# Choosing the eight largest by zeroing them and subtracting the rest on GpSimd, in a convolution, mixture-of-experts and attention kernel

## The chip, the cores and the metric

The kernel runs on one core of a Trainium2 chip. The metric is the device time of one execution in microseconds (us); lower is better. The core has five engines that run side by side, each through its own queue in order: TensorE (PE, with its weight loads shown as PEld), VectorE (DVE), ScalarE (ACT), GpSimd (POOL) and SyncE (SP, which here only starts DMAs). They wait for each other through semaphores.

## The reference, cut to what matters

The input is 32 images of 128 channels and 56 by 56 points. Layer 0 is a depthwise convolution with a mixture of eight experts; the change does not touch it. Layer 1 sees each image as 3136 tokens of 128 channels. It adds an attention over each token's own channels, then a feed-forward part in which each of 64 experts picks its own tokens:

```python
t = t + _L1_attn_ref(_ln_t(t), ...)
# _L1_ffn_ref, with E = 64 experts and K = 8:
logits = jnp.einsum('bsd,ed->bse', x, gate_w) + gate_b
probs = jax.nn.softmax(logits, axis=1)              # over the tokens of one image
vals, idx = jax.lax.top_k(probs.transpose(0, 2, 1), K)
topv = vals.transpose(0, 2, 1)
...
pooled = jnp.einsum('bked,bke->bed', gathered, topv)
...
outputs = outputs.at[jnp.arange(Bn)[:, None], flat_idx].add(weighted)
```

So for every image and expert the eight tokens with the largest probability are needed, with their probabilities, and nothing of the others. The kernel writes this as a mask of 64 by 3136 values per image: the probability where the token is among the eight, and zero elsewhere. The mask, turned by TensorE, weighs the sum over tokens (`pooled`), and it weighs the expert's output again when that is added to the tokens at the very end.

## The kernel before, in words

The attention stage ("block 1") takes 784 tiles of 128 tokens, one in each step of a loop over `k`. A group is 7 tiles, a pair of images is 7 groups, which is 49 steps, and there are 16 pairs. The order of the work on every engine is written out by hand: the objects `pe`, `ve`, `sc` and `gp` tie each instruction behind the one before it on its engine. In step k the text issues, among others:

- `ends` (DVE): two reductions over the keys of two tiles, in every second step; they need `keys` (PE) of those tiles.
- `quotients` (DVE): three small operations, in the other steps.
- `offsets` (DVE): the 128 by 2048 differences `s` of tile k; they need `pivots` (POOL), which makes `c` for two tiles from what `ends` left.
- `scores` (POOL): multiplies `s` of tile k in place. `exps` (ACT) of tile k-1, `values` (DVE: `ev`) and `sums_s` (PE) of tile k-2, `sums_ev` (PE) of tile k-3 follow.

Each step also has two half-steps, calls of `group_work`, one after `keys` and one at the end of the step. They issue the work on whole groups from the table `places`: loading a group's tokens (`load`, by SP), their squares and scaling (`head_*`), the projection (`tail_sum`, `tail_summed`), the turned rows with their squares (`tail_rows`), and the logits (`tail_logits` to `tail_turned`). A place is a number of half-steps counted from the group's first tile. `tail_turned` writes the logits of a pair of images into `lg`, 128 partitions (2 images by 64 experts) by 3136 tokens.

When a pair's logits are complete, the generator `choose` is started, and every half-step runs it up to its next `yield`. In the half-steps counted from its start it does: at 0 DVE takes the eight largest of each row (`max`, into `m8`) and the negated largest; at 2 ACT forms `pb`, the exponentials of `lg` minus the largest, with their sum; at 4 DVE takes the reciprocal, and `match_replace` puts `FAR` (-3e38) into `lg` where the eight values stand; at 6 ACT scales `pb`; at 8 DVE keeps `pb` only where `lg` is below half of `FAR` (one `scalar_tensor_tensor`), and SP stores the mask to DRAM (`mk_d`). From 10 on, ten parts follow, eight half-steps each: PE turns a part of the mask (`cm`), two half-steps later ACT scales it into `mT`, two later PE multiplies it with the tokens (`acc`), three later DVE adds the result into `pT`.

The small PSUM results of the group work and of `choose` share one tag, `tp`, with three buffers; so each of them can start only when the third one before it has been read. SBUF buffers that the change touches: `lg` and `pb` one each of 3136 values per partition, `sq` two (scratch output of the squares), `tr` five and `t2` two.

Of the kernel before, what the change touches and what calls it, by code (L numbers as in the profile page):

```python
# [8 lines left out]
F32 = mybir.dt.float32  # L9
I32 = mybir.dt.int32  # L10
U32 = mybir.dt.uint32
AF = mybir.ActivationFunctionType
ALU = mybir.AluOpType
# [4 lines left out]
P = 128  # L18
GJ = 7
GT = P * GJ  # L20
# [5 lines left out]
def conv_attn_hybrid_kernel(  # L26
# [24 lines left out]
    nc = tc.nc  # L51
    N, C, H, W = x.shape
    HW = H * W
# [15 lines left out]
    E2 = gate_w.shape[0]  # L69
# [14 lines left out]
    mk_d = dram.tile([N, E2, HW], F32, name="mk_d")  # L84
# [31 lines left out]
    def group_rows(d, g):  # L116
        return d[g * GT : (g + 1) * GT, :].rearrange("(j p) c -> p j c", p=P)
# [18 lines left out]
    def by_tile(t):  # L136
        return t.rearrange("c (j p) -> c j p", p=P)
# [61 lines left out]
    with tc.tile_pool(name="cv_c", bufs=1) as cc, tc.tile_pool(  # L199
        name="cv", bufs=3  # L200
# [3 lines left out]
        gp = cc.tile([C, KS, 2 * H], F32, name="gp")  # L204
# [4 lines left out]
        bias = cc.tile([P, C], F32, name="bias")  # L209
# [113 lines left out]
    with tc.tile_pool(name="rt_c", bufs=1) as cc, tc.tile_pool(  # L323
        name="rt", bufs=4
# [72 lines left out]
    with tc.tile_pool(name="sel", bufs=1) as se, tc.tile_pool(  # L397
        name="sel2", bufs=2
# [260 lines left out]
    with tc.tile_pool(name="sc_c", bufs=1) as cc, tc.tile_pool(  # L659
        name="sc", bufs=4  # L660
# [50 lines left out]
        pe, ve, ac = (InOrder(e) for e in (nc.tensor, nc.vector, nc.scalar))  # L711

        def load(g):
            pr, gl = divmod(g, GPP)
            ct = cts[g] = sc.tile([C, GT], F32, name="ct", bufs=5)
            xg = xgs[g] = sc.tile([C, GT], F32, name="xg", bufs=5)
            for im, px, col, n in segments(gl):
                nc.sync.dma_start(
                    xg[:, col : col + n],
                    x[2 * pr + im].rearrange("c h w -> c (h w)")[:, px : px + n],  # L720
                )
                nc.sync.dma_start(ct[:, col : col + n], conv_d[2 * pr + im, :, px : px + n])
# [91 lines left out]
    with tc.tile_pool(name="ex_w", bufs=2) as ew, tc.tile_pool(  # L814
        name="ex", bufs=3
# [37 lines left out]
        gp = InOrder(nc.gpsimd)  # L853
# [3 lines left out]
        for i, (e, b) in enumerate(blocks):  # L857
# [15 lines left out]
            xa, rows, n = got.pop(i)  # L873
# [48 lines left out]
    keep = ctx.enter_context(tc.tile_pool(name="keep", bufs=1))  # L922
    pT = keep.tile([C, E2, N], F32, name="pT")
    NT = NG * GJ
    FAR = -3.0e38
    with tc.tile_pool(name="at_c", bufs=1) as cc, tc.tile_pool(
        name="at", bufs=2
    ) as at, tc.tile_pool(name="at_p", bufs=2, space=PSUM) as atp:
# [6 lines left out]
            return atp.tile([P, 4, P], F32, name=name, tag="tp", bufs=3)  # L935


        wr = at.tile([C, 3 * C], F32, name="wr", tag="lg", bufs=1)
        nc.sync.dma_start(wr, w_qkv)
        ps = bank("p_w")[:, :3, :].rearrange("p a c -> p (a c)")  # L940
        nc.tensor.matmul(ps, turn, wr, start=True, stop=True)
# [41 lines left out]
        pe, ve, sc, gp = (InOrder(e) for e in (nc.tensor, nc.vector, nc.scalar, nc.gpsimd))  # L983

        def squares(src, ss):

            sq = at.tile([P, C], F32, name="sq", bufs=2)
            sc.activation(sq[:, : C - 1], src[:, : C - 1], AF.Square, accum_out=ss)


# [61 lines left out]
        trs, zrs, roots, qs_, oTs, t2s, us, lgt = ({} for _ in range(8))  # L1052
# [101 lines left out]


        def load(g):
            tr = trs[g] = at.tile([P, GJ, C], F32, name="tr", bufs=5)
            nc.sync.dma_start(tr, group_rows(t_d, g))

        def head_squares(g, j0, j1):  # L1160
# [53 lines left out]
        def tail_summed(g, j0, j1):  # L1214
            pr, gl = divmod(g, GPP)
            if j0 == 0:
                t2s[g] = at.tile([C, GT], F32, name="t2")
            t2, ps = t2s[g], held.pop(("t", g, j0))
            sc.activation(by_tile(t2)[:, j0:j1, :], ps[:, : j1 - j0, :], AF.Identity, bias=bp)
            if j1 == GJ:  # L1220
                for im, px, col, n in segments(gl):
                    nc.sync.dma_start(t2_d[2 * pr + im, :, px : px + n], t2[:, col : col + n])
# [44 lines left out]
        def tail_turned(g, j0, j1):  # L1267
            pr, gl = divmod(g, GPP)
            if gl == 0 and j0 == 0:
                lgt[pr] = at.tile([2 * E2, HW], F32, name="lg", bufs=1)  # L1270
            ps = held.pop(("g", g, j0))
            for im, px, col, n in segments(gl):
                c0, c1 = max(col, j0 * P), min(col + n, j1 * P)
                if c0 < c1:
                    e = slice(im * E2, (im + 1) * E2)
                    sc.activation(
                        lgt[pr][e, px + c0 - col : px + c1 - col],
                        ps.rearrange("p j t -> p (j t)")[e, c0 - j0 * P : c1 - j0 * P],
                        AF.Identity, bias=gb[e, :],
                    )  # L1280
            if j1 == GJ:
                aT = at.tile([GJ, P], F32, name="aT", bufs=2)
                sc.copy(aT, ps[:GJ, 3, :])
                nc.sync.dma_start(
                    al_d[g * GT : (g + 1) * GT].rearrange("(j p) -> j p", p=P), aT
                )
# [3 lines left out]
        def choose(pr):  # L1290
            lg = lgt.pop(pr)
            m8 = at.tile([2 * E2, 8], F32, name="fm8")
            ve.max(m8, lg)
            sm = at.tile([2 * E2, 3], F32, name="fsm")
            ve.tensor_scalar(sm[:, 0:1], m8[:, 0:1], -1.0, None, ALU.mult)
            yield
            yield
            pb = at.tile([2 * E2, HW], F32, name="pb", bufs=1)
            sc.activation(pb, lg, AF.Exp, bias=sm[:, 0:1], accum_out=sm[:, 1:2])
            yield  # L1300
            yield
            ve.reciprocal(sm[:, 2:3], sm[:, 1:2])
            ve.match_replace(lg, m8, lg, FAR)
            yield
            yield
            sc.activation(pb, pb, AF.Copy, scale=sm[:, 2:3])
            yield
            yield
            ve.scalar_tensor_tensor(pb, lg, 0.5 * FAR, pb, ALU.is_lt, ALU.mult)
            nc.sync.dma_start(mk_d[2 * pr : 2 * pr + 2].rearrange("n e t -> (n e) t"), pb)  # L1310
            yield
            yield
            for im in range(2):
                e = slice(im * E2, (im + 1) * E2)
                parts = [(gl, *s[1:]) for gl in range(GPP) for s in tile_parts(gl) if s[0] == im]
                px = 0
                for gi, (gl, j0, j1, p) in enumerate(parts):
                    u, r = us[pr * GPP + gl]
                    pn, nj = p.stop - p.start, j1 - j0
                    ps = atp.tile([P, GJ, E2], F32, name="cm", tag="tp", bufs=3)  # L1320
                    for j in range(nj):
                        pe.transpose(
                            ps[:pn, j, :], pb[e, px + j * pn : px + (j + 1) * pn], ident[e, e]
                        )
                    px += nj * pn
                    yield
                    yield
                    mT = at.tile([P, GJ, E2], F32, name="mT", bufs=1)
                    if p.start:
                        sc.copy(mT[p, :nj], ps[:pn, :nj])  # L1330
                    for j in range(nj):
                        sc.activation(
                            mT[p, j], mT[p, j] if p.start else ps[p, j], AF.Copy,
                            scale=r[p, j0 + j : j0 + j + 1],
                        )
                    yield
                    yield
                    ps = atp.tile([P, E2], F32, name="acc", tag="tp", bufs=3)
                    for j in range(nj):
                        pe.matmul(  # L1340
                            ps, u[p, j0 + j, :], mT[p, j, :], start=(j == 0), stop=(j == nj - 1)
                        )
                    yield
                    yield
                    yield
                    if gi == 0:
                        ve.tensor_copy(pT[:, :, 2 * pr + im], ps)
                    else:
                        ve.tensor_tensor(
                            pT[:, :, 2 * pr + im], pT[:, :, 2 * pr + im], ps, ALU.add  # L1350
                        )
                    yield
# [2 lines left out]

        first, last, whole = (0, 4), (4, GJ), ()
        places = [
            (-43, load, whole),
            (-27, head_squares, (0, 2)), (-26, head_squares, (2, 4)),
            (-25, head_squares, (4, 6)), (-24, head_squares, (6, GJ)),  # L1360
            (-15, head_scale, (0, 2)), (-14, head_scale, (2, 4)), (-13, head_scale, (4, GJ)),
# [60 lines left out]
    with tc.tile_pool(name="f_c", bufs=1) as cc, tc.tile_pool(  # L1422
        name="f", bufs=3
    ) as fp, tc.tile_pool(name="f_p", bufs=2, space=PSUM) as fps, tc.tile_pool(
        name="o", bufs=2
# [59 lines left out]
        nc.sync.dma_start(fo_d, so)  # L1485
        nc.sync.dma_start(outF[:E2], fo_d.rearrange("n e c -> e n c"))

        OC = 448
        for n in range(N):
            mk = op.tile([E2 + 1, HW], F32, name="mk")  # L1490
            nc.sync.dma_start(mk[:E2], mk_d[n])  # L1491
# [1 line left out]
            t2 = op.tile([C, HW], F32, name="to")  # L1493
            nc.sync.dma_start(t2, t2_d[n])
            ot = op.tile([C, HW], F32, name="oo", bufs=2)
            for c0 in range(0, HW, OC):
                ps = fps.tile([C, OC], F32, name="p_o", bufs=3)
                nc.tensor.matmul(ps, outF[:, n, :], mk[:, c0 : c0 + OC], start=True, stop=True)  # L1498
                nc.vector.tensor_tensor(ot[:, c0 : c0 + OC], t2[:, c0 : c0 + OC], ps, ALU.add)  # L1499
            nc.scalar.dma_start(out[n].rearrange("c h w -> c (h w)"), ot)  # L1500
# [30 lines left out]
```

## Time and profile before

| what | value |
|---|---|
| median of 3 runs | 10098.04 us (10097.11 to 10102.77) |
| the profiled execution, its own time | 9671.71 us |
| its span, first to last instruction | 9670.0 us |
| mean granted TensorE clock | 0.941 |
| attention stage, its steady part, 4500 to 9048 us | 4548 us |
| busy in it: PE, DVE, POOL, ACT | 4270.2, 4299.7, 4184.6, 3639.4 us |

The profile is of one execution, which was shorter than the three timed ones. In the profile nearly every operation of this stage has line L161, since the helper that ties the instructions together issues them; they are told apart by the names of their tiles. An entry such as `s<-s,q 128x2048` reads: writes `s`, reads `s` and `q`, on 128 partitions by 2048 elements. `[0.96 <-DVE s L161]` after an entry says that the engine stood idle for 0.96 us before it and that the end of DVE's work on `s` released it.

### The profile page before, as it was taken

What the parts mean: (1) busy time and instruction counts of PE and PEld (TensorE: products, weight loads), DVE (VectorE), ACT (ScalarE), POOL (GpSimd) and SP (SyncE); (2) the same over time, 40 slices, a digit from 0 to 9 for tenths busy, and PEclk for the clock granted to TensorE, in tenths of its full rate; (3) what the DMA queues carried; (4) which work ended last, traced back from release to release, by engine and by line L of the source; (5) the groups of instructions that cost most, each with busy time, mean ns of one, the idle gap of its engine ahead of it and who ended that gap; (6) DMA issues with size and microseconds to landing.
All of it is one profiled execution on the core that took longest, in us unless ns stands there. A gap on an engine that the chain in (4) does not pass through costs nothing. (4 is left out here: it accounts for less than half of the span.)

```text
span 9670.0 us, 165492 instructions
## 1 busy us (share of the span) xinstructions
PE 8710.9 (90%) x62536; PEld 7091.7 (73%) x62536; DVE 6485.0 (67%) x10965; ACT 5264.1 (54%) x13385; POOL 6776.2 (70%) x4884
## 2 busy tenths in 40 slices
PE   9999467777999999997999999999999999999888
PEld 3449445555766666666898888898888898888853
DVE  2127888885222222227999999999999999999423
ACT  1116633333333333336887778878787887778400
POOL 0002147777877778778999999999999999999300
PEclk9999789998999999999999999999999999999765
DMA  9984147775444444441000000000000000000389
GB/s 210 214 196 145 56 130 208 208 209 146 74 66 71 70 65 63 65 68 28 31 24 31 31 29 29 31 24 31 31 31 27 31 24 31 31 29 27 95 275 332
DMA packets 1019567, 849.92 MB, mean 88 GB/s; under 512 B 525876, under 2 KB 912247, under 8 KB 999250
## 3 DMA queue, kind: packets, MB, share of 16 engines
q1 hardware_dynamic: 464018, 479.57, 17.4%
q0 software_dynamic: 177664, 188.81, 10.9%
q10 hardware_dynamic: 377088, 170.96, 6.5%
q8 instruction: 495, 8.11, 0.4%
q14 instruction: 302, 2.47, 0.1%
HBM read 486.34 MB, written 353.64 MB: 87 GB/s over the span
## 5 line engine op out<-in xcount | busy, mean ns | idle before, releaser
L161 POOL TENSOR_TENSOR s<-s,q 128x2048 f32<-128x2048 f32 x784 | 3598.9, 4596 | 205.6 <-DVE s L161 172.3
L161 ACT ACTIVATE s<-s 128x2048 f32<-128x2048 f32 x784 | 1501.6, 1915 | 871.2 <-POOL s L161 867.3
L161 POOL DMA_INDIRECT t_d<-ys,xe x992 | 1530.6, 1543 | 408.6 <-issue 230.2
L161 DVE TENSOR_TENSOR s<-kv,c 128x2048 f32<-128x2048 f32 x784 | 1788.6, 2281 | 7.4 <-POOL c L161 7.4
L161 DVE TENSOR_TENSOR ev<-s,kv 128x2048 f32<-128x2048 f32 x784 | 1785.7, 2278 | 1.9 <-ACT s L161 1.9
L161 PE MATMUL sm<-ident,ev 128*128 128x128 f32 x12544 | 1544.0, 278 | 109.6 <-DVE ev L161 109.3
L161 PE MATMUL sm<-ident,s 128*128 128x128 f32 x12544 | 1531.2, 276 | 8.1 <-ACT s L161 8.1
L161 PEld LDWEIGHTS sm<-ident,ev 128*128 128x128 f32 x12544 | 1429.5, 144 | 124.0 <-DVE ev L161 121.5
L161 PEld LDWEIGHTS sm<-ident,s 128*128 128x128 f32 x12544 | 1412.9, 143 | 28.3 <-ACT s L161 8.6
L888 ACT ACTIVATE hT<-ph,b1t 128x512 f32<-128x512 f32 (+1 forms) x992 | 679.3, 685 | 1238.8 <-PE ph L884 1223.4
L899 DVE TENSOR_TENSOR ys<-py,b2t 128x512 f32<-128x512 f32 (+1 forms) x248 | 171.5, 692 | 1527.7 <-PE py L894 1441.2
L894 PEld LDWEIGHTS py<-w,hT 128*128 128x128 f32 x7936 | 956.8, 192 | 202.4 <-issue 92.1
L884 PE MATMUL ph<-xeT,w 128*128 128x512 f32 (+1 forms) x1984 | 923.3, 599 | 70.5 <-DVE xeT L880 70.5
L894 PE MATMUL py<-w,hT 128*128 128x128 f32 x7936 | 980.7, 277 | 0.1
L697 POOL DMA_INDIRECT xb_d<-xs,rd x784 | 766.2, 977 | 240.2 <-issue 202.3
L241 PE MATMUL cps<-xin,br 56*64 56x448 f32 x7168 | 683.0, 539 | 13.0 <-DVE br L235 11.2
L884 PEld LDWEIGHTS ph<-xeT,w 128*128 128x128 f32 x1984 | 349.2, 191 | 393.3 <-issue 293.7
L161 PE MATMUL pa<-rw,ct 128*128 128x256 f32 x1568 | 423.1, 414 | 204.8 <-DVE xs L161 204.8
L241 PEld LDWEIGHTS cps<-xin,br 56*64 56x64 f32 x7168 | 282.3, 132 | 413.0 <-issue 410.4
L161 PEld LDWEIGHTS pa<-rw,ct 128*128 128x128 f32 x1568 | 301.3, 204 | 337.1 <-DVE xs L161 249.5
L287 POOL MEMSET code<- 128x64 f32 x1 | 0.2, 151 | 692.3 <-DMA conv_d<-ot 692.3
L161 ACT COPY add<-px 128x512 f32<-128x512 f32 x224 | 119.1, 532 | 607.1 <-PE px L161 589.8
(327 smaller groups left out, 13794.5 us busy)
## 6 DMA issues: line engine op xcount, KB each, us to landing
ct<-conv_d SPq DMA_DIRECT2D x192, 448.0 KB
xin<-in_x_dram SPq DMA_DIRECT2D x256, 196.0 KB
conv_d<-ot ACTq DMA_DIRECT2D x512, 98.0 KB
t_d<-xs ACTq DMA_DIRECT2D x112, 448.0 KB
tr<-t_d SPq DMA_DIRECT2D x112, 448.0 KB
to<-t_d SPq DMA_DIRECT2D x32, 1568.0 KB
out_dram<-oo ACTq DMA_DIRECT2D x32, 1568.0 KB
xg<-in_x_dram SPq DMA_DIRECT2D x96, 448.0 KB
```

What stands on the lines that cost most here:

```text
L161: r = getattr(self.engine, name)(*a, **k)
L241: nc.tensor.matmul(pss[r][b * HP : (b + 1) * HP], br[rows, kw, :], xi[rows, b * NB : (b + 1) * NB, kw : kw + W], start=(kw == 0), stop=(kw ...
L287: nc.gpsimd.memset(code, -1.0)
L697: s = nc.gpsimd.indirect_dma_start(out=xb_d, out_offset=bass.IndirectOffsetOnAxis(ap=idx, axis=0), in_=row, in_offset=None, bounds_check=R ...
L884: nc.tensor.matmul(ph[:, :, :rows], w1[:, f * P : (f + 1) * P], xT[:, :, :rows], start=True, stop=True,)
L888: nc.scalar.activation(hT[:, f, :, :rows], ph[:, :, :rows], AF.Gelu, bias=b1t[:, f : f + 1])
L894: nc.tensor.matmul(py[:rows, j, :], hT[:, f, j, :rows], w2[:, f, :], start=(f == 0), stop=(f == NF - 1),)
L899: nc.vector.tensor_tensor(ys[:rows], py[:rows], across(b2t, SB)[:rows], ALU.add)
```

## The change

The choice is made on the probabilities instead of the logits. ACT puts the eight largest values `m8` through the same exponential and the same scaling as `pb`. DVE's `match_replace` then reads `pb` and writes into `lg` a copy of `pb` in which the eight are zero. GpSimd subtracts that copy from `pb`, in seven parts of 448 columns, which leaves the eight probabilities and zeros. The parts are spread over the half-steps: two before the first part of the mask is turned, the others in pairs just after PE's turns. The store to `mk_d` follows the seventh. DVE's `scalar_tensor_tensor` is gone.

The order inside `choose`, in half-steps from its start, becomes: `max` 0, exponentials 2, reciprocal 4, scaling 5, `match_replace` 7, subtractions at 9, 10, 11, 12, 19, 20 and 27, and the ten parts from 11 on, one half-step later than before. `lg` now has two buffers, as it is read for longer. To make room, `sq` and `t2` have one buffer and `tr` four, and `load` is issued 30 half-steps ahead of its group instead of 43.

```diff
-    FAR = -3.0e38
+    OC = 448
...
-        wr = at.tile([C, 3 * C], F32, name="wr", tag="lg", bufs=1)
+        wr = at.tile([C, 3 * C], F32, name="wr", tag="lg", bufs=2)
...
-            sq = at.tile([P, C], F32, name="sq", bufs=2)
+            sq = at.tile([P, C], F32, name="sq", bufs=1)
...
-            tr = trs[g] = at.tile([P, GJ, C], F32, name="tr", bufs=5)
+            tr = trs[g] = at.tile([P, GJ, C], F32, name="tr", bufs=4)
...
-                t2s[g] = at.tile([C, GT], F32, name="t2")
+                t2s[g] = at.tile([C, GT], F32, name="t2", bufs=1)
...
-                lgt[pr] = at.tile([2 * E2, HW], F32, name="lg", bufs=1)
+                lgt[pr] = at.tile([2 * E2, HW], F32, name="lg", bufs=2)
...
             sc.activation(pb, lg, AF.Exp, bias=sm[:, 0:1], accum_out=sm[:, 1:2])
+            sc.activation(m8, m8, AF.Exp, bias=sm[:, 0:1])
             yield
             yield
             ve.reciprocal(sm[:, 2:3], sm[:, 1:2])
-            ve.match_replace(lg, m8, lg, FAR)
+            yield
+            sc.activation(pb, pb, AF.Copy, scale=sm[:, 2:3])
+            sc.activation(m8, m8, AF.Copy, scale=sm[:, 2:3])
             yield
             yield
-            sc.activation(pb, pb, AF.Copy, scale=sm[:, 2:3])
+            ve.match_replace(lg, m8, pb, 0.0)
             yield
             yield
-            ve.scalar_tensor_tensor(pb, lg, 0.5 * FAR, pb, ALU.is_lt, ALU.mult)
-            nc.sync.dma_start(mk_d[2 * pr : 2 * pr + 2].rearrange("n e t -> (n e) t"), pb)
-            yield
-            yield
+
+            def leave(i):
+
+                if i < HW // OC:
+                    at_ = slice(i * OC, (i + 1) * OC)
+                    gp.tensor_tensor(pb[:, at_], pb[:, at_], lg[:, at_], ALU.subtract)
+                if i == HW // OC - 1:
+                    nc.sync.dma_start(mk_d[2 * pr : 2 * pr + 2].rearrange("n e t -> (n e) t"), pb)
+
+            left = 0
+            while left < 2:
+                leave(left)
+                left += 1
+                yield
...
                     px += nj * pn
+                    leave(left)
+                    left += 1
                     yield
+                    leave(left)
+                    left += 1
                     yield
...
-            (-43, load, whole),
+            (-30, load, whole),
```

More of the change, by code (lines that the diff above doesn't have):

```diff
@@ L924, in conv_attn_hybrid_kernel @@
     NT = NG * GJ
-    FAR = -3.0e38
+    OC = 448
+    assert HW % OC == 0
     with tc.tile_pool(name="at_c", bufs=1) as cc, tc.tile_pool(
@@ L1486, in conv_attn_hybrid_kernel @@
         nc.sync.dma_start(outF[:E2], fo_d.rearrange("n e c -> e n c"))
-        OC = 448
         for n in range(N):
```

## The prediction

> **What bounds the kernel now.** I read the busy times by stretch first. The attention stage's steady part (columns: stretch and length, then busy time and instructions of each engine, granted TensorE clock, DMA share, GB/s):
>
> ```profile
> 4500.00:9048.00 4548.00, 4270.19 (x35134) 4026.30 (x35132) 4299.72 (x3755) 3639.38 (x9057) 4184.57 (x2417) 0.98 0.08 28
> 5649.00:5943.00 294.00, 273.30 (x2239) 257.19 (x2238) 274.47 (x241) 233.34 (x583) 267.12 (x156) 0.98 0.08 29
> ```
>
> The second line is one pair of images. DVE works 274 us of 294, PE 273, POOL 267: three engines near full, none alone the bound. DMA is idle. Pairs last 286.5 and 293.8 us in turn (from one `max` to the next), 290.2 in the mean.
>
> Then the waits, between 5000 and 8000 us (total, times, longest):
>
> ```profile
> ACT s L161 <- POOL s L161: 544.2, 326, 4.5
> DVE kx L161 <- PE kv L161: 139.5, 129, 5.7
> POOL s L161 <- DVE s L161: 120.3, 156, 3.5
> PE sm L161 <- DVE ev L161: 77.1, 32, 3.8
> ```
>
> Nearly all of DVE's idle time, 13.5 us a pair, is `ends` waiting for PE's keys. So away from the choice PE is the last to come. The fourth line shows the reverse, and the timeline places it: PE waits for `ev` where `choose` runs. There DVE is dense and PE and POOL are not:
>
> ```profile
> 5080.00:5106.00 26.00, 19.99 (x142) 18.71 (x141) 25.86 (x22) 19.27 (x52) 21.25 (x9) 0.89 0.26 98
> ```
>
> In this stretch lie `match_replace` and `scalar_tensor_tensor`. The timeline of DVE and POOL around the latter (start, duration, instruction):
>
> ```profile
> 5095.07 2.28 DVE L161 TENSOR_TENSOR s<-kv,c 128x2048 f32<-128x2048 f32 x1
> 5097.27 3.41 DVE L161 SCALAR_TENSOR_TENSOR pb<-lg,pb 128x3136 f32<-128x3136 f32 x1
> 5100.60 2.28 DVE L161 TENSOR_TENSOR ev<-s,kv 128x2048 f32<-128x2048 f32 x1
> ```
> ```profile
> 5091.85 4.58 POOL L161 TENSOR_TENSOR s<-s,q 128x2048 f32<-128x2048 f32 x1 [0.65 <-DVE s L161]
> 5097.50 7.60 POOL L161 TENSOR_TENSOR s<-s,q 128x2048 f32<-128x2048 f32 x1 [1.07 <-DVE s L161]
> ```
>
> Two prices stand here. On DVE the operation takes 5100.60 - 5097.27 = 3.33 us of the queue. And the product on GpSimd that starts beside it takes 7.60 instead of 4.58 us: 3.02 us lost. In the next pair a small product, `c<-q,kx`, takes 3.87 instead of 0.62: 3.25 lost. It is so in all 15 pairs that have work beside them. Beside `max` and `match_replace`, as long but with one input, the products keep 4.5 to 4.6 us.
>
> The last reading is PE's clock after such a gap:
>
> ```profile
> 5963.00:5968.00 5.00, 4.94 (x26) 4.57 (x27) 4.93 (x5) 4.87 (x5) 1.49 (x2) 0.66 0.23 92
> 5968.00:5977.00 9.00, 6.66 (x59) 6.18 (x57) 9.00 (x7) 8.78 (x35) 8.84 (x5) 1.00 0.16 68
> 5977.00:5982.00 5.00, 4.83 (x23) 4.37 (x23) 4.93 (x6) 1.45 (x1) 4.85 (x2) 0.66 0.50 206
> ```
>
> Twice per choice the granted clock falls to half for 3.4 us, once after PE's gap at `match_replace`, once after that at `scalar_tensor_tensor`.
>
> **What the Trainium skill says.** "SBUF — State Buffer", SBUF: two separate sides: a DVE operation with two SBUF inputs and a GpSimd operation that reads SBUF exclude each other for a whole instruction. The 3.0 to 3.25 us above agree; none of DVE's other operations here has two SBUF inputs (their second one is in PSUM), so the subtractions will not be locked out. "GPSIMD Engine Reference", Elementwise — side-by-side cycle accounting: a two-input product of 2048 columns takes 4497 ns on GpSimd, 2293 on DVE; the trace has 4569 (median) and 2281. "TensorE: Matmul & The Clock Gate", What's actually happening: an idle window of about 3.4 us halves PE's clock; the trace shows halves of 3.41 us, after gaps of 2.4 to 3.8 us.
>
> **The change part by part**, per pair, of which 16 are computed and 15 have other work beside them.
>
> *DVE loses `scalar_tensor_tensor`*: -3.33 us. DVE is dense there and PE waits for it (2.45 us idle in that step, 0.9 in the next), so I count it in full: 15 x 3.33 = -50 us. `max` and `match_replace` stay at 3.4 us each; the latter reads `pb` instead of `lg`, same size. What is late next is PE's own work.
>
> *The clock*: without that gap the second halving should go. It costs at most half of 3.41 us, 1.7 us a pair; PE may be hidden behind DVE meanwhile, so I take half, 0.85 x 15 = -13 us, bounds 0 and -26.
>
> *GpSimd gains seven subtractions of 448 columns.* From 0.62 us at 256 columns and 4.56 at 2048: 2.20 ns a column, 1.04 us each, 7.3 us a pair, 7.8 with the issue gaps. The lock's 3.0 to 3.25 us go, so POOL has 4.3 us more: 267 becomes 271 of 290, still under PE's 273. But they come in a bunch. With c the step in which the choice starts, one follows `scores` of step c+4, two that of c+5, one that of c+6: 4.2 us, behind which the `pivots` of steps c+5 and c+7 and later `scores` are queued. From the durations, in one of the two kinds of pair (in the other `pivots` fall one step off): `scores` of c+4 starts 2.43 us after its `offsets`; with 4.57 for each `scores`, 1.6 for `pivots` and 1.04 for each subtraction, POOL ends the `pivots` of step c+7 at 23.6 us after the `offsets` of c+4, where DVE at its usual 5.06 and 5.65 us a step wants them at 21.4. So DVE comes to wait 2.1 us at c+8. In that place it waits now anyway, 1.7 us for PE's keys in one kind of pair and 1.2 one step on in the other: uncovered 0.4 and 0.9. Two more subtractions at c+9 and c+10 are again 2.1 us late; in one kind of pair DVE waits 5.7 us for keys at c+12, in the other only 0.5 at c+13, which leaves 0 and 1.6. The seventh, at c+13, falls into 1 us of POOL's idle time. Mean (0.4 + 0.9 + 0 + 1.6) / 2 = 1.4 us a pair: +21 us. Bounds: 0, as ACT's wait for POOL ends 6 to 8 us before PE takes those tiles and 3 to 4 before DVE does; and all 7.3.
>
> *ACT*: two activations of 8 columns, 0.2 us each (as `st<-st` of 14 columns, 0.214), and `pb`'s scaling a half-step earlier. ACT has 57 us idle a pair, nearly all of it waiting for POOL: 0. `match_replace` waits for that scaling now; DVE reaches it some 7 us after the `exps` ahead of the scaling started, and ACT is through in about 7. Bounds 0 and +1.
>
> *The buffers.* `load` with four buffers cannot start before `tail_sum` of four groups earlier is through on PE. From there to ACT's first square of the group there are 4.0 to 12.2 us now (median 5.8), and the packets of a load have landed 2.8 to 3.7 us after its issue, 4.5 once: 0, with +0.5 us a pair as the upper bound; squares queue `exps` behind them. The load keeps its place in SP's queue between the same stores; the store to `mk_d` moves 19 half-steps later and its reader is 200 us away. One `sq` buffer: successive squares overlap by about 0.06 us now; were each to wait for the last, 98 x 0.06 = 6 us of ACT, under its idle time: 0 to +1. One `t2`: its last reader on PE is two steps ahead of the next writer: 0. Two `lg`: ACT's writes no longer wait for DVE; that wait is not seen among ACT's: 0.
>
> *The ten parts run a half-step later.* The three `tp` buffers then meet other neighbours. The worst now is `acc`, which waits for the squares of `p_u`; after it PE runs at half clock for 6.8 us, and DVE's longest wait for keys follows:
>
> ```profile
> 5724.22 2.63 PE L161 MATMUL acc<-mT,u 128*128 128x64 f32 x14 [2.12 <-ACT sq L161]
> ...
> 5734.15 0.76 DVE L161 TENSOR_REDUCE kx<-kv 128x16 f32<-128x256 f32 x2 [5.71 <-PE kv L161]
> ```
>
> A half-step later `acc` meets the second `p_u`, about 1.3 us behind instead of 2.1. I can't sum that over a pair; 0, bounds -2 and +2 us a pair.
>
> *The last pair* has no cover. Now match and scaling run side by side, then 3.43 us of `scalar_tensor_tensor`. After: 2.9 + 0.4 of scaling ahead of the match, then two subtractions, 2.1: +2 us, once.
>
> Sum: -50 - 13 + 21 + 2 = -40 us. Against the profiled execution's own 9671.7 that gives 9632. The median, 10098.0, is 426 us above that execution, from what the profile does not show; I carry it over unchanged: **10058 us**.
>
> **The rivals.** What 0.2% means: 20 us, about what a measurement of this kernel can tell.
>
> *GpSimd becomes the bound (slower).* The subtractions reach the path in full, since POOL runs at 92% and each `scores` feeds ACT, whose late squares and scalings PE waits for. From the point where POOL is later than the 2.4 us between `pivots`' end and its `offsets`, everything adds: 7.3 - 3.33 = +4.0 us a pair, +60 us: 10158. For it: ACT waits 544 us for POOL. Against: POOL itself waits 120 us for DVE, and idles 23 us a pair.
>
> *PE takes the gain (no change).* PE's work stays at 273 us; in the timed runs, longer than the profiled one, PE may be slower and fuller. Then only what PE idled at the third DVE operation counts, and part is lost to late group work: -5 us, 10093.
>
> *The new order frees more.* Both clock halvings per choice go (-26 instead of -13), the `acc` waits shrink (-2 a pair, -30), subtractions cost 10 instead of 21: -50 - 26 - 30 + 10 + 2 = -94, 10004.
>
> *The change doesn't do what it says*: `match_replace` must find ACT's values bit for bit; if it missed, the time would be the same.
>
> **How the numbers follow.** Forecast 0.55 (its own range 10035 to 10078), GpSimd as bound 0.20, PE takes it 0.17, more freed 0.08. Faster 0.63, same 0.17, slower 0.20. Range 10002 to 10130: it takes in the lower bounds of clock and order, and leaves out most of the slower case and a little below.
>
> **What would show it.** Right: products on POOL without a 7.6 us one; `subtract` at about 1.04 us; PE's gap at c+4 and one halving gone; DVE 271 us a pair, POOL 271; pairs of about 287.5 us. Wrong: DVE's `s` waiting for POOL's `c` by more than 2 us a pair; ACT's `sq` waiting for DMA; PE's waits for ACT's `sq` and `lg` above the present 9.6 us a pair.

## The result and the profile after

The changed kernel takes 10220.1 us (median of 4 runs, 10207.63 to 10234.22), the kernel before beside it 10100.31 (10097.11 to 10102.77). The ratio is 1.0119, with a 95% interval of 1.0102 to 1.0137: 120 us slower, where the prediction had 42 us faster. The profiled execution took 10207.63 us, with a span of 10205.9.

In some comparisons layer 0, which the change does not touch, takes some 420 us longer for both kernels (the first `offsets` starts at 4413.9 us in the profile before, at 4833.5 in the profile after, and at 4423.6 in another profile of the same changed kernel), so below a kernel is held against the runs of before in its own comparison, or by the length of a pair.

"A pair" is from one `max` to the next, as the mean of 14. It was 290.2 us and is 297.2 us. The two kinds of pair, in turn, were 286.5 and 293.8; now they are mostly 292.2 and 301.5. Where a text below speaks of the "second kind", it is the shorter one, of 286.5 us before. That gives 14 x 7.0 = 98 us; the last interval between two `max` went from 213.6 to 225.2 us (+11.6), and the stretch after the last `max` from 611.6 to 614.1 (+2.5). The sum is 112 us: the loss lies in block 1, and nearly all of it in its steady part.

First the busy times by stretch, after (the columns are as in the prediction; the first stretch holds the 14 pairs, the second one pair):

```profile
5206.30:9366.60 4160.30, 3849.52 (x31407) 3606.64 (x31406) 3796.74 (x3347) 3372.89 (x8163) 3800.88 (x2254) 0.98 0.08 28
5498.50:5799.80 301.30, 274.98 (x2228) 257.48 (x2227) 270.64 (x239) 241.19 (x585) 271.27 (x162) 0.97 0.08 28
```

Divided by 14, DVE works 271.2 us a pair and GpSimd 271.5, the two sums that the prediction gave (271 and 271); PE works 275.0, where 273 were taken. DVE's and GpSimd's work is as forecast, and still the pair is 10 us longer than forecast. What grew is waiting: DVE idles 26.0 us a pair instead of 15.7, PE 22.2 instead of 17.4, GpSimd 25.7 instead of 23.2. The question is who waits for whom.

PE's waits for the squares (`sq`) before, in the stretch of 5500 to 8772 us, 11.3 pairs (engine and tile, awaited engine and tile: total us, times, longest):

```profile
PE acc L161 <- ACT sq L161: 29.1, 22, 2.1
PE p_g L161 <- ACT sq L161: 24.8, 23, 1.4
PE p_x L161 <- ACT sq L161: 3.5, 5, 0.7
```

The waits after, in the same stretch, 11 pairs:

```profile
DVE kx L161 <- PE kv L161: 260.6, 157, 6.5
PE p_g L161 <- ACT sq L161: 61.2, 33, 2.7
PE acc L161 <- ACT sq L161: 33.6, 22, 1.6
PE cm L161 <- POOL pb L161: 33.0, 11, 3.7
PE p_x L161 <- ACT sq L161: 26.3, 27, 2.2
PE sm L161 <- DVE ev L161: 25.3, 28, 2.2
ACT sq L161 <- DMA tr<-t_d: 3.1, 5, 1.4
```

DVE's wait for keys has gone from 13.5 to 23.7 us a pair (260.6 / 11): PE is late, and DVE pays. PE's wait for DVE's `ev` fell from 7.0 to 2.3 us a pair; that is in part the gain that was wanted, and in part PE comes later to `ev`. One wait has grown: PE waits for ACT's squares where its small results need a `tp` buffer, 121.1 us in the three lines, 11.0 a pair, against 57.4 us, 5.1 a pair, before. One is new: once a pair PE waits 3.0 us for GpSimd's subtraction (`pb`). The last line clears the loads: 3.1 us of waiting in 11 pairs.

The second wait in the timeline (start, duration, instruction, and in brackets the idle time before it with its releaser). PE:

```profile
6129.51 0.37 PE L161 MATMUL cm<-ident,pb 64*128 64x64 f32 x3 [1.03 <-ACT zT L161]
6133.57 0.69 PE L161 MATMUL cm<-ident,pb 64*128 64x64 f32 x4 [3.69 <-POOL pb L161]
6134.18 3.37 PE L161 MATMUL sm<-ident,ev 128*128 128x128 f32 x16
6137.40 1.03 PE L161 MATMUL kv<-wq,zT 128*128 128x256 f32 x4
```

and GpSimd and DVE in the same stretch:

```profile
6125.20 1.16 POOL L161 TENSOR_TENSOR pb<-pb,lg 128x448 f32<-128x448 f32 x1
6126.32 0.23 POOL L161 TENSOR_TENSOR kx<-kx 128x16 f32<-128x16 f32 x1
6126.62 0.62 POOL L161 TENSOR_TENSOR c<-q,kx 128x256 f32<-128x256 f32 x1
6127.32 0.62 POOL L161 TENSOR_TENSOR c<-c,kx 128x256 f32<-128x256 f32 x1
6127.90 4.52 POOL L161 TENSOR_TENSOR s<-s,q 128x2048 f32<-128x2048 f32 x1
6132.37 2.24 POOL L161 TENSOR_TENSOR pb<-pb,lg 128x448 f32<-128x448 f32 x2
```
```profile
6138.46 0.76 DVE L161 TENSOR_REDUCE kx<-kv 128x16 f32<-128x256 f32 x2 [5.03 <-PE kv L161]
```

The first part of the mask is seven turns of 128 columns. Three of them run at once; the fourth reaches past column 448, so it needs the second subtraction, and that stands on GpSimd behind `pivots` and a product of 4.52 us. PE's order is written out, so `sums_ev` and the next `keys` stand behind those four turns. Then the clock: after the gap the 16 `sm` of 6134.18 take 3.37 us instead of the usual 1.91. The stretches show it (columns as above, the granted clock third from the end):

```profile
6127.00:6130.20 3.20, 1.02 (x7) 0.63 (x7) 3.13 (x5) 2.27 (x8) 3.12 (x3) 1.00 0.00 0
6130.20:6133.50 3.30, 0.00 (x0) 0.00 (x0) 3.23 (x2) 1.05 (x1) 3.30 (x3) 0.51 0.00 0
6133.50:6137.10 3.60, 3.53 (x18) 3.42 (x19) 0.00 (x0) 3.22 (x11) 3.60 (x3) 0.50 0.00 1
```

DVE does nothing in the third one. The clock is at half from 6130.3 to 6137.1 us. It falls 0.4 us after the gap of 3.69 us has begun: ahead of the fall lie shorter gaps of 1.01 and 1.03 us, and in the first stretch PE is busy for only 1.02 of 3.20 us. So the long gap did not start the half clock; PE idled through most of its first 3.4 us and paid in the second. The Trainium skill ("TensorE: Matmul & The Clock Gate", What's actually happening) speaks of an idle window of about 3.4 us; the halves here last 3.4 or 6.8 us, but a gap need not be that long: in the prediction's lines half clock follows the gap of 2.12 us before `acc` at 5724.22. Over a pair, PE's time at half clock went from 11.7 to 14.6 us: the halving at `scalar_tensor_tensor` has gone, and others have come.

The first wait, for the squares, shows best in ACT's own timeline. Before:

```profile
5098.75 0.28 ACT L161 ACTIVATE sq<-p_u 128x127 f32<-128x127 f32 x1
5098.91 0.20 ACT L161 ACTIVATION_READ_ACCUMULATOR sq<-p_u 128x1 f32 x1
5099.01 0.28 ACT L161 ACTIVATE sq<-p_u 128x127 f32<-128x127 f32 x1
```

and after:

```profile
6119.54 0.28 ACT L161 ACTIVATE sq<-p_u 128x127 f32<-128x127 f32 x1
6119.71 0.20 ACT L161 ACTIVATION_READ_ACCUMULATOR sq<-p_u 128x1 f32 x1
6119.94 0.28 ACT L161 ACTIVATE sq<-p_u 128x127 f32<-128x127 f32 x1
```

The durations are the same; the starts are 0.26 us apart before and 0.40 after. With two scratch buffers a square starts 0.10 us ahead of the end of its forerunner's accumulator read; with one it starts only behind that end. In the median a square of `p_u` follows the last by 0.249 us before and by 0.399 after, one of `tr` by 0.292 and 0.433. There are 70 such successions in a pair: 10 us of ACT's time. Of this, 7.4 us show as busy time (240.9 us a pair, 233.5 in `a_sq2`, below, which has two buffers): the squares no longer overlap the reads ahead of them.

Two more lines, from the list of the costliest groups and from the groups of the 11 pairs (instructions, then busy us, mean ns, idle before):

```profile
L161 POOL TENSOR_TENSOR s<-s,q 128x2048 f32<-128x2048 f32 x784 | 3576.2, 4566 | 228.9 <-DVE s L161 153.0
L161 POOL TENSOR_TENSOR pb<-pb,lg 128x448 f32<-128x448 f32 x77 | 87.9, 1148 | 0.0
```

The product locked out for 7.6 us has gone, as predicted: the longest is now 4.6 us. A subtraction takes 1.15 us where 1.04 was worked out.

### The profile page after: what moved, and what is told of

Its sections match the earlier page's. It is cut to its first block, busy times and chain, and to the rows that moved or that the text cites. A ratio compares the mean times of both kernels' runs of the same rounds, so it can differ in the third digit from the quotient of the medians.

```text
span 10205.9 us, 165596 instructions
## 1 busy us (share of the span) xinstructions
PE 8830.4 (87%) x62536; PEld 7165.0 (70%) x62536; DVE 6441.3 (63%) x10949; ACT 5391.5 (53%) x13417; POOL 6849.7 (67%) x4996
## 4 chain that ended last, share of the span: by engine, by line
PE 45%; DVE 17%; POOL 15%; ACT 9%; issue 6%; DMA 4%; another core or an unknown queue 3%; SPq 0%; POOLq 0%; ACTq 0%; DVEq 0%
POOL s L161 10%; PE sm L161 9%; PE ph L884 7%; PE cps L241 6%; PE py L894 6%; DVE s L161 4%; DVE ev L161 3%; ACT sq L161 3%; ACT s L161 3%; PE pa L161 2%; DMA to<-t_d 2%; PE pc L364 2%; PE pl L377 2%; PE acc L161 2%
## 5 line engine op out<-in xcount | busy, mean ns | idle before, releaser
L161 PE MATMUL sm<-ident,ev 128*128 128x128 f32 x12544 | 1577.0, 281 | 38.2 <-DVE ev L161 37.9
L161 PE MATMUL pa<-rw,ct 128*128 128x256 f32 x1568 | 486.1, 461 | 528.8 <-DVE xs L161 467.3
L161 PEld LDWEIGHTS pa<-rw,ct 128*128 128x128 f32 x1568 | 345.7, 231 | 677.7 <-DVE xs L161 497.8
L161 DVE SCALAR_TENSOR_TENSOR xs<-pa,rst,add 128x256 f32<-128x256 f32 x784 | 352.5, 481 | 543.7 <-remote 400.1
```

The costliest lines, as they stand in the source:

```text
L161: r = getattr(self.engine, name)(*a, **k)
```

## The experiments

Two theories stood against each other from the start: the loss is GpSimd's (its seven subtractions reach PE), or it is the one `sq` buffer's. The second was in no rival of the prediction.

**The `sq` buffer, from both sides.** `a_sq2` is the changed kernel with two `sq`; to make room, the small `al` gets one buffer. `before_sq1` is the kernel before with one `sq`.

```diff
-            sq = at.tile([P, C], F32, name="sq", bufs=1)
+            sq = at.tile([P, C], F32, name="sq", bufs=2)
...
-                al = held["a", g] = at.tile([P, GJ], F32, name="al", bufs=2)
+                al = held["a", g] = at.tile([P, GJ], F32, name="al", bufs=1)
```

> The changed kernel (10220 us) with two buffers for the squares' scratch tile sq again; 32 bytes for it come from al, which gets one buffer instead of two. Theory 1 (squares): with one buffer each square on ACT waits for the one before it, 0.40 us from start to start instead of 0.25, which is 0.15 x 98 = 15 us of ACT a pair, and PE's small results wait for it; of the 7 us that a pair became longer plus the 3.4 us that DVE should have won, 10.3 us, about 6.5 are due to it. Expected: squares 0.25 us apart again, PE's p_g waits for ACT's sq back from 5.6 to about 2 us a pair, pairs of about 290.5 us, 10120 us. Theory 2 (PE waits for GpSimd's subtraction before the first part of the mask, and nothing else): 10220 us. Rival 3 (GpSimd's load of 7.3 us a pair is the bound): 10220 us. Rival 4 (the ten parts a half-step later are the cause): 10220 us.

Measured: 9708.91 us against 9676.68, ratio 1.0033 (1.0021 to 1.0046); 291.7 us a pair. The squares are 0.25 us apart again, but `p_g` still waits 4.6 us a pair for them, where about 2 were forecast. In `before_half_later`, below, it waits 4.4 us with two `sq` buffers and nothing changed but the half-step, and in the kernel before 2.1: that part of the wait belongs to the half-step.

> The kernel before (10100 us) with one buffer for sq and nothing else changed. Theory 1: squares 0.40 us apart, pairs longer by 3 to 6.5 us, 10145 to 10200 us. Theories 2 to 4: 10100 us, as nothing else of the change is in it.

Measured: 9763.36 us against 9676.68, ratio 1.0092 (1.0077 to 1.0108); 295.6 us a pair. The squares are 0.40 us apart here too, and PE's waits in this kernel, in the stretch of 5500 to 8772 us, are:

```profile
PE acc L161 <- ACT sq L161: 39.8, 22, 2.7
PE p_g L161 <- ACT sq L161: 35.4, 22, 1.9
PE p_x L161 <- ACT sq L161: 13.1, 19, 2.3
```

The same three in `a_sq2`, with the wait for GpSimd:

```profile
PE p_g L161 <- ACT sq L161: 53.6, 35, 2.2
PE cm L161 <- POOL pb L161: 32.9, 11, 3.7
PE acc L161 <- ACT sq L161: 17.5, 17, 1.1
PE p_x L161 <- ACT sq L161: 12.5, 19, 1.6
```

The two answers agree: 297.2 - 291.7 = 5.5 us a pair with the change (the one `al` is in this figure too), 295.6 - 290.2 = 5.4 without it. All of PE's waits for ACT together, over the 14 pairs, fall from 16.9 to 12.1 us a pair with the second buffer and grow from 10.3 to 15.3 without it: 4.8 and 5.0 us, nearly the whole price. So of the loss of 7.0 us a pair, some 5.4 is one number in one line, and it has nothing to do with the choice. The wait for `pb` is the same with two `sq` (32.9 against 33.0), so it belongs to the rest.

**The wait for the first two subtractions.** `a_early2` is the changed kernel with the first two subtractions straight behind `match_replace`, at half-step 7 instead of 9 and 10; the ten parts stay at 11.

```diff
             ve.match_replace(lg, m8, pb, 0.0)
-            yield
-            yield
...
             left = 0
             while left < 2:
                 leave(left)
                 left += 1
-                yield
+            yield
+            yield
+            yield
+            yield
```

> The changed kernel with the first two subtractions issued right behind match_replace, ahead of the scores of step c+4, where GpSimd stands idle for 3.5 us; the ten parts stay at half-step 11. Theory 2: PE's first turn of the mask no longer waits for GpSimd (33 us in 11 pairs now), DVE's waits for keys at c+6 and c+7 of 5.1 and 2.8 us go, 3.8 us a pair: 10163 us. Theory 1: 10220 us. Rival 3: 2.2 us of load a pair move into idle time, 10187 us, and PE's wait was no cause. Rival 4: 10220 us.

Measured: 9775.55 us against 9676.68, ratio 1.0107 (1.0091 to 1.0122); 296.2 us a pair. PE's wait for `pb` is gone from its waits, but the pair is only 1.0 us shorter. A wait of 3.0 us on the engine that is last was worth a third of that.

`a_sq2_early2_h10` has two `sq` besides (and one `al`; those lines are as in `a_sq2`), and the parts at half-step 10, where they were before.

```diff
...
+            ve.match_replace(lg, m8, pb, 0.0)
             left = 0
             while left < 2:
                 leave(left)
                 left += 1
-                yield
+            yield
+            yield
+            yield
```

> The changed kernel with all three undone: two sq buffers (one for al), the first two subtractions right behind match_replace, and the ten parts at half-step 10 as before. If theories 1 and 2 together hold all of the loss, DVE's 3.33 us a pair show at last: pairs of 286.5 to 288 us, 10045 to 10065 us, faster than both kernels. Rival 3 (GpSimd's load): not below 10120 us. If something else is in it, above 10100 us.

Measured: 9707.88 us against 9676.68, ratio 1.0033 (1.0021 to 1.0045); 292.1 us a pair, as `a_sq2`. With the price of one `sq` paid back and the first wait removed, it is still 1.9 us a pair slower than before.

**The changed kernel once more**, beside the next three, as the yardstick of that comparison:

> The changed kernel unaltered, on one chip with the runs of this call, so that it can be set beside them: its pairs of images took 297.2 us against 290.2. If the loss lies in the attention stage alone, 16 pairs and the last one's tail, it is again 105 to 125 us slower than the kernel before, whatever the earlier stages take.

Measured: 9786.46 us against 9677.5, ratio 1.011 (1.0095 to 1.0126); 297.1 us a pair. It repeats: +109 us here, +120 in the first comparison.

**What the removed DVE operation is worth.** `before_no_mask` is the kernel before without it:

```diff
-            ve.scalar_tensor_tensor(pb, lg, 0.5 * FAR, pb, ALU.is_lt, ALU.mult)
```

> The kernel before without the scalar_tensor_tensor: DVE's 3.33 us and GpSimd's 3.0 us of lock-out are gone and nothing is put in their place (left out: the masking, so that every token's probability goes on). This is the most that the change could win. Theory of the prediction (DVE's time there counts in full): pairs of 286.9 us, -50 us. Rival (PE is the bound of the whole pair and makes up the time behind the choice anyway): pairs of 289 to 290 us, -5 to -20 us.

Measured: 9648.05 us against 9677.5, ratio 0.9971 (0.996 to 0.9982); 288.5 us a pair, between the two forecasts. Of 3.33 us taken out of a dense stretch of DVE, 1.7 us reach the end in the old order, and PE's time at half clock falls only from 11.7 to 11.2 us a pair. The rest is given back within the pair: DVE's wait for keys grows by 1.6 us a pair. PE's wait for `ev` falls by 2.3 us, not by the 4.7 of the changed kernel. That this is the most the change could win did not hold, as the next run shows.

**What the subtractions are worth.** `a_sq2_no_sub` is `a_sq2_early2_h10` without them:

```diff
-                    gp.tensor_tensor(pb[:, at_], pb[:, at_], lg[:, at_], ALU.subtract)
+                    pass
```

> As a_sq2_early2_h10, whose pairs took 292.1 us, without the seven subtractions on GpSimd (left out: the subtraction, so that every token's probability goes on). Theory: GpSimd's lateness behind the subtractions at half-steps 10, 11, 18 and 19 reaches PE through ACT at steps c+9 to c+13, about 4 us in one kind of pair and 1 to 3 in the other: without them 288 us or less a pair, about -40 us against the kernel before. Rival (the later match_replace and the earlier scaling cost it): 292 us still.

Measured: 9634.37 us against 9677.5, ratio 0.9952 (0.9939 to 0.9966); 287.0 us a pair. So what the change takes away is worth 3.2 us a pair (290.2 - 287.0) in the new order, net of the change's other parts. Of the 1.5 us by which this beats `before_no_mask`, 1.3 are PE's busy time (270.9 against 272.2), as PE's time at half clock is 8.0 us a pair instead of 11.2. The seven subtractions cost 292.1 - 287.0 = 5.1 us, where they add 7.4 us to GpSimd's busy time (271.4 against 264.0). On PE, 2.7 of the 5.1 us are waiting, and 2.4 are the same work at half clock for longer.

Where they bite is seen at one `acc` of the second kind of pair. In `a_sq2_no_sub`:

```profile
5436.32 1.77 PE L161 MATMUL acc<-mT,u 128*128 128x64 f32 x14 [0.60 <-ACT sq L161]
```

In `a_sq2_early2_h10`, GpSimd, ACT and PE ahead of what I take to be the same `acc` (71.0 and 75.5 us after the pair's `max`):

```profile
5437.19 2.24 POOL L161 TENSOR_TENSOR pb<-pb,lg 128x448 f32<-128x448 f32 x2
5440.97 9.07 POOL L161 TENSOR_TENSOR s<-s,q 128x2048 f32<-128x2048 f32 x2
```
```profile
5445.57 1.91 ACT L161 ACTIVATE s<-s 128x2048 f32<-128x2048 f32 x1 [2.47 <-POOL s L161]
5447.38 0.57 ACT L161 COPY u<-p_u 128x512 f32<-128x512 f32 x1
5447.85 0.28 ACT L161 ACTIVATE sq<-p_u 128x127 f32<-128x127 f32 x1
```
```profile
5449.05 3.25 PE L161 MATMUL acc<-mT,u 128*128 128x64 f32 x14 [3.83 <-ACT sq L161]
```

Read it from the bottom. `acc` waits 3.83 us for squares of `p_u`, whose `tp` buffer it takes. The squares stand on ACT behind `exps`, and `exps` waited 2.47 us for its product. Right ahead of the product, and of the `pivots` between them, stand two subtractions. After the gap `acc` runs at half clock, 3.25 us instead of 1.77. At this place the subtractions cost PE 3.83 - 0.60 + 3.25 - 1.77 = 4.7 us, although ACT's wait for GpSimd ended "6 to 8 us before PE takes those tiles": PE does not wait for the tile of `exps` but for the squares behind it in ACT's queue.

**The half-step.** `before_half_later` is the kernel before with the ten parts one half-step later:

```diff
             yield
             yield
+            yield
             for im in range(2):
```

> The kernel before with one more half-step ahead of the ten parts, as in the changed kernel; nothing else. The prediction took this for 0, with 2 us a pair either way. Theory (squares and GpSimd's lateness hold the loss): within 1 us a pair, 10 to 15 us either way. Rival (the order of the small results is what costs): 2 us a pair and more, +30 us.

Measured: 9689.0 us against 9677.5, ratio 1.0011 (1.0005 to 1.0018); 290.9 us a pair. That is +0.7 us, with PE's time at half clock at 15.1 us instead of 11.7. The half-step alone would explain the halvings but hardly any of the time: a good part of half clock lies under DVE's work.

**Amount or place?** If each subtraction costs by its place, another placement would keep the 3.2 us. Five kernels vary `a_sq2_early2_h10` (subtractions 0 to 6 at half-steps 7, 7, 10, 11, 18, 19, 26). The first runs only the last three of them:

```diff
-                if i < HW // OC:
+                if 4 <= i < HW // OC:
```

> As a_sq2_early2_h10 (two sq, match_replace and two subtractions at half-step 7, the ten parts from 10 on), but the first four of the seven subtractions are left out, so in columns 0 to 1791 the mask keeps every probability; the last three, behind PE's turns at half-steps 18, 19 and 26, stay. Theory A (GpSimd's lateness is what costs, and the three late ones cost at c+10 to c+13 as much as the bunch at the front): pairs of 289.5 us, half-way between 287.0 without any and 292.1 with all, 9671 us. Theory B (the four at the front make the delay, the rest fits into GpSimd's idle time): 287.3 us, 9638 us. Theory C (the late ones make it all): 291.5 us, 9700 us.

Measured: 9676.61 us against 9681.15, ratio 0.9995 (0.9987 to 1.0003); 289.7 us a pair. The first theory holds: three of the seven subtractions cost 2.7 of the 5.1 us.

The next kernels move the subtractions. The first of them has three at half-step 7 and the rest one place earlier; the second has them apart (its lines that issue a subtraction when its half-step is due are left out here and below):

```diff
-            while left < 2:
+            while left < 3:
```

> As a_sq2_early2_h10, with one more subtraction at once behind match_replace (three at half-step 7) and the other four one place earlier, at 10, 11, 18 and 19: none is left at 26. Theory A (what counts is the amount of GpSimd's work, wherever it lies): 292.1 us a pair, 9707 us. Theory B (the one at half-step 26, ahead of the second image's parts, costs on its own): 291 us, 9692 us.

Measured: 9721.99 us against 9681.15, ratio 1.0038 (1.0025 to 1.0052); 291.9 us a pair.

```diff
...
+            due = {7: (0, 1, 2), 10: (3,), 13: (4,), 16: (5,), 24: (6,)}
```

> As a_sq2_early2_h10, with the subtractions apart: three at half-step 7, then one each at 10, 13, 16 and 24, each still ahead of the turn that reads it. Theory A (amount of work counts, GpSimd has no slack near the choice): 292.1 us a pair, 9707 us. Theory B (the pairs of them, 2.3 us in one gap between two products, count; single ones of 1.15 us fit into the 1.6 us that GpSimd idles a step): 289 us, 9665 us, under before.

Measured: 9711.2 us against 9681.15, ratio 1.0032 (1.002 to 1.0045); 291.8 us a pair. Both speak for the amount and against the place: breaking up the couples gains nothing.

```diff
...
+            due = {7: (0, 1, 2), 12: (3,), 20: (4,), 22: (5,), 28: (6,)}
```

> As a_sq2_spread, but the later ones as late as their turns allow: three at half-step 7, then 12, 20, 22 and 28. Theory A (amount): 292.1 us a pair, 9707 us. Theory B (pairs of them count, singles fit): 289 us, 9665 us. If only the region of half-steps 10 to 20 is dense, this one is quicker than a_sq2_spread by 1 us a pair, 15 us.

Measured: 9676.51 us against 9681.15, ratio 0.9998 (0.999 to 1.0006); 290.1 us a pair. That speaks for the place, up to a point: the same seven cost 3.1 us instead of 5.1. The loss at c+12 and c+13 of the second kind of pair (5.7 us in `a_sq2_early2_h10`) is gone, and one of 2.6 us at c+7 has come, which `a_sq2_early2_h10` did not have. So the last run puts together the two halves that lose nothing:

```diff
-            due = {7: (0, 1, 2), 12: (3,), 20: (4,), 22: (5,), 28: (6,)}
+            due = {7: (0, 1), 12: (2,), 15: (3,), 20: (4,), 22: (5,), 28: (6,)}
```

> As a_sq2_late, with only two subtractions at half-step 7 and the third and fourth apart, at 12 and 15; the last three stay at 20, 22 and 28. a_sq2_late took 290.1 us a pair, 3.1 over the same kernel with no subtractions (287.0): of this 1.3 lies at step c+7 of the second kind of pair, where a_sq2_early2_h10, with two at half-step 7, lost nothing; and a_sq2_late loses nothing at c+12 and c+13, where a_sq2_early2_h10 lost 2.9 (mean over both kinds). Theory A (GpSimd's subtractions cost where they put a product later than its squares' turn on ScalarE, so place by place): both losses go, 288.5 us a pair, 9654 us, quicker than before by 0.25%. Theory B (what is spared in one place is paid in another, since GpSimd's 7.8 us have nowhere to go): 290 us, 9676 us, as before.

Measured: 10089.61 us against 10092.69, ratio 0.9997 (0.9989 to 1.0005); 290.1 us a pair. The forecast of a gain fell. Step by step, held against `a_sq2_no_sub`, the 2.6 us at c+7 have gone as meant, but 1.4 us have come at c+6 of the first kind of pair (which `a_sq2_late` had 1.6 us shorter) and 2.2 us in c+11 to c+13 of the second. At c+12 of the first kind, where `a_sq2_late` lost 2.0 us that the text above does not name, nothing is lost now. The two new losses make 1.8 us of the mean; the rest lies mostly from c+17 on and was not followed up. The place decides 2 of the 5.1 us; the other 3.1 stayed in both of these placements, about what the removed DVE operation was worth. That no placement can save them is not shown. No placement tried is quicker than the kernel before; `a_sq2_late` and `a_sq2_late2` are equal to it.

## Why the prediction was wrong

Two terms of its sum failed: one `sq` buffer, put at 0 to +1 us a pair, cost 5.4, and the subtractions, put at +1.4, cost about 5. Per pair the kernels stand at 290.2 (before), 287.0 (`a_sq2_no_sub`), 291.7 (`a_sq2`) and 297.2 us (after): -3.2 for what is taken away in the new order, +4.7 for the subtractions as the change places them, +5.5 for one `sq`, +7.0 together. These add up by construction, and the second difference holds the half-step too; what supports the split is that the `sq` price is 5.4 in the kernel before as well, and that the subtractions cost 5.1 with the parts at half-step 10. Point by point:

- *DVE loses `scalar_tensor_tensor`, -3.33 us in full, and the clock, -0.85*: together -4.2 predicted, -1.7 (old order) to -3.2 (new order) measured. The mechanism was there: without the operation PE's wait for `ev` falls by 2.3 us a pair in the old order. "I count it in full" was too much: what PE gains in one step, DVE partly waits out for keys later. The clock's gain came only without the subtractions: half clock fell by 3.7 us a pair in `a_sq2_no_sub`, and rose by 2.9 in the changed kernel. The prediction's "gaps of 2.4 to 3.8 us" before a halving was also too narrow, as its own gap of 2.12 us before `acc` shows.
- *One `sq` buffer, "98 x 0.06 = 6 us of ACT, under its idle time: 0 to +1"*: this is the step that failed most. The overlap was read from the squares alone, and the accumulator read, the second instruction of each square, was left out: the starts move by 0.15 us, and 70 of them make 10 us of ACT a pair. And "under its idle time" was wrong in kind. ACT's 57 us of idle time lie in its waits for products; the squares lie just behind `exps`, where PE waits for them. Cost: 5.4 us a pair.
- *GpSimd's subtractions, +1.4*: 4.7 to 5.1 measured. The mechanism taken, lateness through `pivots`, was nearly absent: DVE's wait for `c` is not among its waits in the changed kernel, and 0.8 us a pair in `a_sq2_early2_h10`. The subtractions came to PE by two ways that the step did not price. One is new: PE's turns wait for the subtraction itself, 3.0 us once a pair, with `keys` behind them; removing that wait gained 1.0 us. The other is an old one that the prediction put at zero, from product over `exps` and squares to PE. The upper bound, all 7.3, did hold it.
- *Loads, `t2`, ACT's small operations*: nothing speaks against them. ACT waits 0.3 us a pair for DMA, within the bound of 0.5; `t2` and the small operations were not tried alone, but they are in `a_sq2_no_sub`, the kernel with the shortest pairs. *The half-step*: 0 taken, bounds -2 and +2, 0.7 measured. *The last pair*: +2 predicted, the stretch after the last `max` grew by 2.5. That may be chance: the same stretch grew by 3.6 in the repeat of the changed kernel and by nothing in `a_sq2`.
- *No lock-out*: right. The Trainium skill ("SBUF — State Buffer", SBUF: two separate sides) had DVE's operations with two SBUF inputs and GpSimd's exclude each other; with none of the former left, no product in the profile after is over 4.6 us.

Of the rivals, "GpSimd becomes the bound" (+4.0 us a pair, 10158) came nearest, and its reason, "late squares and scalings PE waits for", was the right one; with two `sq` and the change's order the measured net is +1.5. Neither it nor the range of 10002 to 10130 reached 10220, since the `sq` price was in no case. Of what the prediction named as a sign that it was wrong, the third came true: PE's waits for ACT's `sq` and `lg` went from 9.8 to 13.0 us a pair.

## What to carry to other kernels

A scratch buffer that nobody reads can still order the instructions that write it, here at 5.4 us a pair: before it is cut to make room, look at the start-to-start distance of successive writers, accumulator reads included, and at who waits for the last of a bunch. An engine's idle time need not cover added work: here 57 us of idle time on ACT did not cover 10. Ask for each addition what stands behind it in its queue, and behind that in the next engine's queue. Where three engines work over 90% of a loop, work that is moved from one to another may cost on the second all that it saved on the first: here 3.3 us of DVE were worth 3.2 at best, clock included, and 7.4 us of GpSimd cost 3.1 in the best placement tried.

## What the runs showed that was not expected

- Squares with an accumulator, of 127 columns on ACT, follow each other by 0.249 us with two scratch buffers and by 0.399 us with one.
- A GpSimd subtraction of 448 columns takes 1.148 us, where interpolating between the 0.62 us of 256 columns and the 4.56 of 2048 gave 1.04.
- More time at half clock need not cost its whole amount: `before_half_later` has 3.4 us a pair more of it than the kernel before and is 0.7 us a pair slower.
- The granted clock fell to half after a gap of 2.12 us (`acc` at 5724.22 before), and 0.4 us into a gap of 3.69 us (at 6130.3 after), ahead of which lay two gaps of 1.0 us.
